# The first tile's row lookup, transposition and mean in a gathered expert FFN: two other orders of the same work

## The chip, the cores and the metric

The kernel runs on one core of a Trainium2 chip. The metric is the device time of one execution in microseconds (us). The core has five engines that each work through an instruction list of their own in order: TensorE (PE in the profile; its weight loads are listed apart as PEld), VectorE (DVE), ScalarE (ACT), GpSimd (POOL) and SyncE (SP). Transfers are issued by an engine's queue (here SP for the matrices, POOL for gathers and scatters by row number) and carried by 16 shared DMA engines. An engine waits for another, or for a transfer's landing, by semaphores.

## The reference

`x` is 4 x 512 tokens of 512 numbers, so 2048 rows. There are two stages.

```python
x = x + tanh(g_xattn) * moe(layernorm(x), ids, ctx)     # ctx[e]: the 512x512 matrix of expert e, used as Wg, Wu and Wd
x = x + tanh(g_ffn)   * ffn(layernorm(x), w1, w3, w2, wr)
```

In the first stage a token's expert (0 to 3) follows from its id alone, by the bounds 6250, 12500 and 18750. With its matrix M a normed row h gives `z = h M^T`, then `g = silu(z) * z`, then `y = g M^T`; all three weights are the same matrix. The second stage has three dense layers and adds gated rows of all tokens into 8 rows, one per route.

## The kernel before, in words

**Tiling.** Rows are sorted by expert into passes of 128 rows, 17 passes in all: 13 whole ones, each of one expert, and 4 mixed ones of four strips of 32 rows. `order` lists them; it begins 0, 1, 2, 3, 4. In this text x_p, m_p, h_p, z_p, g_p and y_p are the tiles of pass p: gathered rows, expert's matrix (1 MB), centred rows, and the products. The kernel is written with a manual schedule: each engine issues in the order of the program text, and a tile is waited for where it is first used.

**Sorting, L120 to L300.** DVE works out, for every token, its place among the sorted rows (`place`, L246; `padded`, L249), and splits it in a lane 0..127 (`lanes`, L251) and the pass's first place (`inpass`, L253). `which0` (L245) is the matrix of pass 0 alone, ready before the rest. The token number of every lane and pass is then found with matmuls: `atlane` (L258; columns 0..11 by `at_lane(0)`, columns 12..15 by `at_lane(1)`) has a one where a token sits in a lane, `what` (L267, L270; 128 x 17 x 16) has the token's number + 1 where it sits in a pass, and 16 matmuls (L276) add their products into `tok`, 128 lanes x 17 passes, in PSUM. `from_row` (L286) is `tok` as row numbers to gather. `later`, `stepped` and `which` (L287 to L300) give the matrix number of every pass, and `row_tables()` (L308 to L323, called at L836, behind them) gives `to_row` and `first`, seven short DVE instructions. PE meanwhile runs matmuls of ones whose results nobody reads, `busy(10)` before the lookup and `busy(21)` behind it (L200).

**Start of the passes, L846 on.** `load(p)` (L430) has SP read the pass's matrix number from SBUF and start the 1 MB transfer of m_p (L443). `gather(p)` (L387, DMA at L389) has POOL start the gather of x_p by `from_row`. Pass 0's matrix number is read from `which0`; the others are read from `held`, a copy of `which` that POOL makes (L849 for pass 1 alone, L854 for the rest). POOL's list at this place is: gather 0, copy for pass 1, gathers 1, 2, 3 and 4, copy for the rest. SP's list is: m_0, m_1 (which waits for the first copy), m_2 (which waits for the second copy), two loads of gates, m_3.

**First pass, `first_in` (L412).** DVE takes mean and variance of x_0 (L415, L417), subtracts the mean from each half of the columns (L422), PE transposes each half (L427), ACT copies it out of PSUM to hT (L428). `up` (L461) then multiplies: z_0 in four k steps of two matmuls each (L453), and between the third and the fourth k step PE transposes the next pass's centred rows (`turn_in`, L407, by L380 and L410). Behind z, ACT takes silu (L466) and DVE multiplies (L467), both with the row's inverse root `rs`, which `scale` makes in nine dependent DVE instructions on 128 x 1 numbers (L355 to L373). `centre(p)` (L397) is the mean and variance of a pass (L340, L342) and the subtraction (L401).

**Behind that** PE alternates the up and down products of the passes (L453) with transpositions (L380), fed by the same loads and gathers, and then the second stage's layers (L622, L730).

Of the kernel before, what the change touches and what calls it, by code (L numbers as in the profile page):

```python
# [19 lines left out]
P = 128  # L20
# [5 lines left out]
def tile_gated_moe_ffn(  # L26
# [40 lines left out]
    nc = tc.nc  # L67
    NT, D = x.shape
# [3 lines left out]
    KC = D // P  # L72
    NJ = NT // P
# [13 lines left out]
    work = ctx.enter_context(tc.tile_pool(name="work", bufs=3))  # L87
    small = ctx.enter_context(tc.tile_pool(name="small", bufs=4))
    ps_mm = ctx.enter_context(tc.tile_pool(name="ps_mm", bufs=2, space=bass.MemoryType.PSUM))
    ps_x = ctx.enter_context(tc.tile_pool(name="ps_x", bufs=2, space=bass.MemoryType.PSUM))  # L90
    ps_y = ctx.enter_context(tc.tile_pool(name="ps_y", bufs=1, space=bass.MemoryType.PSUM))
# [5 lines left out]
    on_the_way = {  # L97
        "lane", "atlane12", "atlane4", "passes", "what", "place", "over", "rank_in", "incl",
        "keep", "cum", "hot", "before", "later", "stepped", "behind", "ones", "place0", "number",
        "idt", "pad", "psum", "padded", "lanes", "inpass",  # L100
    }

    def ct_(shape, dtype, name):
        if name in on_the_way:
            return pos.tile(list(shape), dtype, tag=name, name=name)
        return const.tile(list(shape), dtype, tag=name, name=name)


    idt = ct_([P, NJ], I32, "idt")
# [28 lines left out]
    for e in range(1, E):  # L138
# [12 lines left out]
    H = 12  # L151
# [5 lines left out]
    number = ct_([P, NJ], F16, "number")  # L157
    nc.gpsimd.iota(
        number, pattern=[[1, NJ]], base=1, channel_multiplier=NJ,
# [13 lines left out]
    ident = ct_([P, P], F32, "ident")  # L173
# [66 lines left out]
    start = ct_([P, 2 * E - 1], F32, "start")  # L240
# [6 lines left out]
    padded = ct_([P, NJ], I16, "padded")  # L247
# [8 lines left out]
    def at_lane(h):  # L256
        j, n = (0, H) if h == 0 else (H, NJ - H)
        return nc.vector.tensor_tensor(  # L258
            atlane[h],
            lane[:, :, 0:n],  # L260
            lanes[:, j : j + n].unsqueeze(1).to_broadcast([P, P, n]),
            ALU.is_equal,
        )

    at_lane(0)
    what = ct_([P, NP, NJ], F16, "what")
    nc.vector.tensor_tensor(  # L267
        what, passes, inpass.unsqueeze(1).to_broadcast([P, NP, NJ]), ALU.is_equal
# [1 line left out]
    nc.vector.tensor_tensor(  # L270
        what, what, number.unsqueeze(1).to_broadcast([P, NP, NJ]), ALU.mult
    )
    at_lane(1)
    tok = ps_x.tile([P, NP], F32, tag="x", name="tok")
    for j in range(NJ):
        nc.tensor.matmul(  # L276
# [4 lines left out]
    later = ct_([P, 2 * E, NU], F32, "later")  # L281
    stepped = ct_([P, 2 * E - 1, NU], F32, "stepped")

    busy(21)
    from_row = ct_([P, NP], I32, "from_row")
    nc.vector.tensor_scalar(from_row, tok, -1.0, 0.0, ALU.add, ALU.max)  # L286
    nc.vector.tensor_tensor(  # L287
# [50 lines left out]
    def moments(xt, name):  # L338
        st = small.tile([P, 6], F32, tag="st", name=f"st_{name}")
        nc.vector.bn_stats(st, xt)  # L340
        mv = small.tile([P, 2], F32, tag="mv", name=f"mv_{name}")
        nc.vector.bn_aggr(mv, st)  # L342
        return mv
# [43 lines left out]
    def gather(p):  # L387
        xt = xp.tile([P, D], F32, tag="x", name=f"x_{p}")
        nc.gpsimd.indirect_dma_start(  # L389
            out=xt,  # L390
            out_offset=None,
            in_=x,
            in_offset=bass.IndirectOffsetOnAxis(ap=from_row[:, p : p + 1], axis=0),
        )
        xs[p] = xt

    def centre(p):  # L397

        mvs[p] = moments(xs[p], f"a{p}")
        hs[p] = work.tile([P, D], F32, tag="h", bufs=4, name=f"h_a{p}")  # L400
        nc.vector.tensor_scalar(hs[p], xs[p], mvs[p][:, 0:1], None, ALU.subtract)  # L401

    def scale(*ps):
        for p, rs in zip(ps, inverse_roots([mvs.pop(p) for p in ps], [f"a{p}" for p in ps])):
            rss[p] = rs
# [5 lines left out]

    def first_in(p):  # L412

        st = small.tile([P, 6], F32, tag="st", name=f"st_a{p}")
        nc.vector.bn_stats(st, xs[p])  # L415
        mvs[p] = small.tile([P, 2], F32, tag="mv", name=f"mv_a{p}")
        nc.vector.bn_aggr(mvs[p], st)  # L417
        hTs[p] = work.tile([P, KC * P], F32, tag="hT", bufs=2, name=f"hT_{p}")
        n = D // 2
        for i in range(2):  # L420
            h = work.tile([P, n], F32, tag="h", bufs=4, name=f"h_a{p}_{i}")
            nc.vector.tensor_scalar(  # L422
                h, xs[p][:, i * n : (i + 1) * n], mvs[p][:, 0:1], None, ALU.subtract
            )
            tp = ps_tp.tile([P, n], F32, tag="tp", name=f"tp_a{p}_{i}")
            for k in range(n // P):
                nc.tensor.transpose(tp[:, k * P : (k + 1) * P], h[:, k * P : (k + 1) * P], ident)  # L427
            nc.scalar.copy(hTs[p][:, i * n : (i + 1) * n], tp)  # L428

    def load(p):  # L430

# [413 lines left out]

    load(order[0])  # L846
    gather(order[0])
    one = slice(order[1], order[1] + 1)
    nc.gpsimd.tensor_copy(held[0:1, one], which[0:1, one])  # L849
    load(order[1])  # L850
    for i in range(1, 5):
        gather(order[i])
    rest = slice(order[1] + 1, NU)
    nc.gpsimd.tensor_copy(held[0:1, rest], which[0:1, rest])  # L854
    first_in(order[0])
    scale(order[0])
    centre(order[1])
    scale(order[1])
    load(order[2])
    nc.sync.dma_start(gates[:, 0:1], g_xattn.to_broadcast([P, 1]))  # L860
    nc.sync.dma_start(gates[:, 1:2], g_ffn.to_broadcast([P, 1]))
    load(order[3])
    up(order[0], inside=lambda: turn_in(order[1]))
    centre(order[2])
    scale(order[2])
    up(order[1], inside=lambda: turn_mid(order[0]))
    turn_in(order[2])
# [95 lines left out]
```

## Time and profile before

| what | value |
|---|---|
| median of 8 runs | 277.31 us (277.15 to 278.14) |
| the profiled execution: its own time | 277.26 us |
| its span, first to last instruction | 275.6 us |
| PE busy | 267.0 us, 97% of the span |
| DVE / ACT / POOL busy | 148.5 / 69.3 / 39.2 us |
| share of PE in the chain that ended last | 94% |
| mean granted TensorE clock | 0.996 |
| first matmul of z_0 | 15.13 us |

The profiled execution lies 0.05 us under the median, and 1.66 us of its time lie around its span. The timeline's columns are: start in us, duration in us, engine, line, operation, result<-operands, shapes, count, and in brackets the idle time of the engine just before and what ended it. Of a transfer started by a queue, the trace also has the landing: one record from each of the 16 DMA engines; a tile is usable when the last of them is in. In this trace the last records come, for m_0, at 11.47 us; for x_0 at 12.79, x_1 at 15.90, m_1 at 19.07, x_2 at 19.39, x_3 at 20.03, x_4 at 20.66 and m_2 at 24.32.

### The profile page before, as it was taken

How to read it: one execution, taken by the hardware profiler on the slowest of the kernel's cores; microseconds unless marked ns; L12 is line 12 of the kernel's file. 1: busy time of each engine (PE TensorE's matmuls, PEld its weight loads, DVE VectorE, ACT ScalarE, POOL GpSimd, SP SyncE). 2: the span in 40 equal slices, each digit the busy share in tenths (PEclk: the TensorE clock that was granted, in tenths of full speed). 3: DMA queues.
4: the chain of work that ended last, by engine and by line, in shares of the span. 5: the costliest groups of instructions: out<-in, count | busy, mean ns of one | idle time of the engine just before them, and what ended most of it. 6: DMA issues, size and time to landing. Idle time of an engine off the chain costs nothing.

```text
span 275.6 us, 3562 instructions
## 1 busy us (share of the span) xinstructions
PE 267.0 (97%) x1173; PEld 125.4 (46%) x1173; DVE 148.5 (54%) x593; ACT 69.3 (25%) x134; POOL 39.2 (14%) x63
## 2 busy tenths in 40 slices
PE   5889999999999999999999999999999999999994
PEld 2445455544355454444344444534345444344362
DVE  6687877877888779918263481516253620711000
ACT  2022232232233231233142232312113233301120
POOL 5520122221122211211110010101010000000000
PEclk9999999999999999999999999999999999999998
DMA  0797999545679996696213093001000000000000
GB/s 1 218 337 270 408 399 366 173 172 186 228 224 402 406 408 244 204 406 237 101 39 152 4 339 152 38 0 40 0 12 2 0 0 1 0 0 2 0 0 2
DMA packets 20722, 42.54 MB, mean 154 GB/s; under 512 B 2143, under 2 KB 2207, under 8 KB 20704
## 3 DMA queue, kind: packets, MB, share of 16 engines
q1 hardware_dynamic: 17952, 33.66, 34.3%
q0 software_dynamic: 2720, 8.65, 8.4%
q8 instruction: 9, 0.15, 0.2%
q14 instruction: 9, 0.07, 0.1%
q10 hardware_dynamic: 32, 0.01, 0.0%
HBM read 38.10 MB, written 4.47 MB: 154 GB/s over the span
## 4 chain that ended last, share of the span: by engine, by line
PE 94%; DVE 2%; DMA 2%; issue 1%; ACT 0%; DVEq 0%
PE z L453 22%; PE y L453 21%; PE v L730 20%; PE X L622 10%; PE Y L622 5%; PE tp_f L380 3%; PE tp_a L380 3%; PE tp_g L380 3%; PE Z L622 2%; PE acc L742 1%; PE lg L699 1%; DMA x<-in_x_dram,from_row 1%; DMA idt<-in_ids_dram 1%; PE accT L758 1%; PE o L814 0%
## 5 line engine op out<-in xcount | busy, mean ns | idle before, releaser
L453 PE MATMUL z<-m,hT 128*32 128x512 f32 (+1 forms) x232 | 61.9, 595 | 0.2 <-ACT hT L428 0.2
L453 PE MATMUL y<-m,gT 128*32 128x512 f32 (+1 forms) x232 | 61.4, 594 | 0.0
L730 PE MATMUL v<-w,s 128*128 128x512 f32 (+1 forms) x136 | 57.3, 570 | 0.0
L730 PEld LDWEIGHTS v<-w,s 128*128 128x128 f32 x136 | 25.0, 190 | 27.2 <-issue 26.7
L453 PEld LDWEIGHTS z<-m,hT 128*32 128x32 f32 (+1 forms) x232 | 22.6, 146 | 29.6 <-issue 28.1
L453 PEld LDWEIGHTS y<-m,gT 128*32 128x32 f32 (+1 forms) x232 | 22.6, 146 | 27.8 <-issue 27.8
L482 POOL DMA_INDIRECT out_dram<-x,to_row x17 | 17.2, 1010 | 86.2 <-DVE x L481 84.4
L389 POOL DMA_INDIRECT x<-in_x_dram,from_row x17 | 16.7, 980 | 76.0 <-DVE h_a L401 34.9
L467 DVE SCALAR_TENSOR_TENSOR g<-z,rs_a,g 128x512 f32<-128x512 f32 x17 | 12.8, 751 | 27.3 <-ACT g L466 27.3
L466 ACT ACTIVATE g<-z,rs_a 128x512 f32<-128x512 f32 x17 | 11.7, 687 | 51.3 <-PE z L453 51.0
L481 DVE SCALAR_TENSOR_TENSOR x<-y,tg,x 128x512 f32<-128x512 f32 x17 | 12.8, 750 | 18.9 <-PE y L453 18.9
L738 ACT ACTIVATE s<-v 128x512 f32<-128x512 f32 (+1 forms) x17 | 9.7, 572 | 41.9 <-PE v L730 41.9
L515 ACT COPY hT<-tp_f 128x512 f32<-128x512 f32 x13 | 7.6, 586 | 43.6 <-PE tp_f L380 43.6
L622 PE MATMUL X<-T,S 128*128 128x512 f32 x32 | 15.0, 592 | 0.0
L340 DVE BATCH_NORM_STATS2 st_a<-x 128x6 f32<-128x512 f32 x16 | 11.0, 687 | 5.0 <-DMA x<-in_x_dram,from_row 5.0
L380 PEld LDWEIGHTS tp_f<-ident,h_f 128*128 128x128 f32 x68 | 8.2, 141 | 10.2 <-issue 10.2
L340 DVE BATCH_NORM_STATS2 st_f<-x 128x6 f32<-128x512 f32 x17 | 11.8, 695 | 0.6
L380 PEld LDWEIGHTS tp_a<-ident,h_a 128*128 128x128 f32 x64 | 7.7, 141 | 9.4 <-issue 9.1
L640 DVE TENSOR_TENSOR s<-X,c 128x512 f32<-128x512 f32 x4 | 2.8, 692 | 16.2 <-PE X L622 16.2
L473 ACT COPY gT<-tp_g 128x512 f32<-128x512 f32 x17 | 10.0, 586 | 5.0 <-PE tp_g L380 5.0
L380 PE MATMUL tp_f<-ident,h_f 128*128 128x128 f32 x68 | 10.4, 276 | 0.0
L380 PE MATMUL tp_g<-ident,g 128*128 128x128 f32 x68 | 10.2, 273 | 0.0
(165 smaller groups left out, 271.8 us busy)
## 6 DMA issues: line engine op xcount, KB each, us to landing
m<-in_ctxT_dram SPq DMA_DIRECT2D x29, 1024.0 KB
w<-in_w1T_dram SPq DMA_DIRECT2D x1, 1024.0 KB
w<-in_w3T_dram SPq DMA_DIRECT2D x1, 1024.0 KB
w<-in_w2T_dram SPq DMA_DIRECT2D x1, 1024.0 KB
x<-in_x_dram,from_row POOLq DMA_INDIRECT x17, 6.0
out_dram<-x,to_row POOLq DMA_INDIRECT x17, 6.0
wr<-in_wrT_dram SPq DMA_DIRECT2D x1, 64.0 KB
x_first<-out_dram SPq DMA_DIRECT2D x4, 4.0 KB
```

Source lines behind the costliest of these rows:

```text
L340: nc.vector.bn_stats(st, xt)
L380: nc.tensor.transpose(tp[:, k * P : (k + 1) * P], h[:, k * P : (k + 1) * P], ident)
L389: nc.gpsimd.indirect_dma_start(out=xt, out_offset=None, in_=x, in_offset=bass.IndirectOffsetOnAxis(ap=from_row[:, p : p + 1], axis=0),)
L453: nc.tensor.matmul(out_ps[i * n : (i + 1) * n, :], lhs[:, k * P + i * n : k * P + (i + 1) * n], m[:, k, :], start=(k == 0), stop=(k == KC ...
L466: nc.scalar.activation(g, z, AF.Silu, scale=rs)
L467: nc.vector.scalar_tensor_tensor(g, z, rs, g, ALU.mult, ALU.mult)
L473: nc.scalar.copy(gT, tp)
L481: nc.vector.scalar_tensor_tensor(xt, y, tg[:, 0:1], xt, ALU.mult, ALU.add)
L482: nc.gpsimd.indirect_dma_start(out=out, out_offset=bass.IndirectOffsetOnAxis(ap=to_row[:, p : p + 1], axis=0), in_=xt, in_offset=None, bou ...
L622: nc.tensor.matmul(out_ps, a[:, k, c * P : (c + 1) * P], bb[:, k, :], start=start and k == 0, stop=k == 1, skip_group_check=True,)
L730: nc.tensor.matmul(v, s1[:, k, c_b + t * P : c_b + (t + 1) * P], w3[:, k, c0 : c0 + n], start=(k == 0), stop=(k == KC - 1),)
L738: nc.scalar.activation(s2, v, AF.Silu)
```

## The change

Two things are done in another way, and some of the work around them is put in another order.

1. The row numbers of pass 0 get a lookup of their own, ahead of the one for all passes. A 128 x 16 instruction makes `what0`, sixteen matmuls of one column make `tok0`, and a 128 x 1 instruction makes `from_row0`, by which gather 0 goes. The lookup for all 17 passes stays whole and comes behind it: its two instructions `what` now stand behind `from_row0` on DVE, its sixteen matmuls behind those of `tok0` on PE. The matmuls of ones behind it go from 21 to 11.
2. `first_in` transposes x_0 as it was gathered, and ACT copies the result to `raw`. DVE sums each row of x_0 (`total`), one matmul against the identity brings the sums, one per token, to all partitions of PSUM (`spread`), and two DVE instructions add `raw` and `spread` times -1/512 into hT, one for each half. Mean and variance of x_0, still needed for the inverse root, are taken behind that.
3. POOL's list becomes: gather 0, gather 1, copy for pass 1, gathers 2, 3, 4, copy for the rest. On DVE the order becomes: centre 1, inverse root of 0, centre 2, [g_0], inverse roots of 1 and of 2, [g_1]; before it was: root of 0, centre 1, root of 1, [g_0], centre 2, root of 2, [g_1]. SP's list, PE's order of products and ACT's list stay as they are.

```diff
+    what0 = ct_([P, NJ], F16, "what0")
+    nc.vector.scalar_tensor_tensor(what0, inpass, 0.0, number, ALU.is_equal, ALU.mult)
+    at_lane(1)
+    tok0 = ps_x.tile([P, 1], F32, tag="x", name="tok0")
+    for j in range(NJ):
+        nc.tensor.matmul(
+            tok0, atlane[j // H][:, :, j % H], what0[:, j : j + 1], start=(j == 0), stop=(j == NJ - 1)
+        )
+    from_row0 = ct_([P, 1], I32, "from_row0")
+    nc.vector.tensor_scalar(from_row0, tok0, -1.0, 0.0, ALU.add, ALU.max)
     what = ct_([P, NP, NJ], F16, "what")
...
-    at_lane(1)
     tok = ps_x.tile([P, NP], F32, tag="x", name="tok")
...
-    busy(21)
+    busy(11)
...
-            in_offset=bass.IndirectOffsetOnAxis(ap=from_row[:, p : p + 1], axis=0),
+            in_offset=bass.IndirectOffsetOnAxis(
+                ap=from_row0 if p == order[0] else from_row[:, p : p + 1], axis=0
+            ),
...
     def first_in(p):
-        st = small.tile([P, 6], F32, tag="st", name=f"st_a{p}")
-        nc.vector.bn_stats(st, xs[p])
-        mvs[p] = small.tile([P, 2], F32, tag="mv", name=f"mv_a{p}")
-        nc.vector.bn_aggr(mvs[p], st)
-        hTs[p] = work.tile([P, KC * P], F32, tag="hT", bufs=2, name=f"hT_{p}")
         n = D // 2
+        raw = work.tile([P, KC * P], F32, tag="h", bufs=4, name=f"raw_{p}")
         for i in range(2):
-            h = work.tile([P, n], F32, tag="h", bufs=4, name=f"h_a{p}_{i}")
-            nc.vector.tensor_scalar(
-                h, xs[p][:, i * n : (i + 1) * n], mvs[p][:, 0:1], None, ALU.subtract
-            )
             tp = ps_tp.tile([P, n], F32, tag="tp", name=f"tp_a{p}_{i}")
             for k in range(n // P):
-                nc.tensor.transpose(tp[:, k * P : (k + 1) * P], h[:, k * P : (k + 1) * P], ident)
-            nc.scalar.copy(hTs[p][:, i * n : (i + 1) * n], tp)
+                c = i * n + k * P
+                nc.tensor.transpose(tp[:, k * P : (k + 1) * P], xs[p][:, c : c + P], ident)
+            nc.scalar.copy(raw[:, i * n : (i + 1) * n], tp)
+        total = small.tile([P, 1], F32, tag="total", name="total")
+        nc.vector.tensor_reduce(total, xs[p], AX.X, ALU.add)
+        spread = ps_y.tile([P, P], F32, tag="y", name="spread")
+        nc.tensor.matmul(spread, total.to_broadcast([P, P]), ident, start=True, stop=True)
+        hTs[p] = work.tile([P, KC * P], F32, tag="hT", bufs=2, name=f"hT_{p}")
+        for i in range(2):
+            half = slice(i * n, (i + 1) * n)
+            nc.vector.scalar_tensor_tensor(
+                hTs[p][:, half].rearrange("p (k t) -> p k t", t=P),
+                spread.unsqueeze(1).to_broadcast([P, n // P, P]),
+                -1.0 / D,
+                raw[:, half].rearrange("p (k t) -> p k t", t=P),
+                ALU.mult,
+                ALU.add,
+            )
+        mvs[p] = moments(xs[p], f"a{p}")
...
     load(order[0])
     gather(order[0])
     one = slice(order[1], order[1] + 1)
+    gather(order[1])
     nc.gpsimd.tensor_copy(held[0:1, one], which[0:1, one])
     load(order[1])
-    for i in range(1, 5):
+    for i in range(2, 5):
         gather(order[i])
...
     first_in(order[0])
+    centre(order[1])
     scale(order[0])
-    centre(order[1])
-    scale(order[1])
+    centre(order[2])
     load(order[2])
...
     up(order[0], inside=lambda: turn_in(order[1]))
-    centre(order[2])
+    scale(order[1])
     scale(order[2])
     up(order[1], inside=lambda: turn_mid(order[0]))
```

More of the change, by code (lines that the diff above doesn't have):

```diff
@@ L99, in tile_gated_moe_ffn @@
         "keep", "cum", "hot", "before", "later", "stepped", "behind", "ones", "place0", "number",
-        "idt", "pad", "psum", "padded", "lanes", "inpass",
+        "idt", "pad", "what0", "psum", "padded", "lanes", "inpass",
     }
```

## Prediction

> **What bounds the kernel now.** The first view is the chain that ended last: PE holds 94% of it. The second is that chain in order of time over the first 30 us, for where it isn't PE:
>
> ```profile
> 7.86 1.00 PE tok L276 x16
> 9.35 3.44 DMA x<-in_x_dram,from_row
> 12.81 0.70 DVE st_a L415
> 13.76 0.36 DVE h_a L422
> 14.26 0.42 PE tp_a L427 x2
> 14.71 0.38 ACT hT L428
> 15.13 2.84 PE z L453 x6
> 17.97 0.44 PE tp_a L380 x4
> 18.41 3.61 PE z L453 x8
> 22.02 0.44 PE tp_g L380 x4
> ```
>
> Up to 15.13 us a chain of short steps decides. From there PE runs on; behind 20 us I find no distance between matmul starts that tells of a wait until the last microseconds. So whatever moves the start of z_1 moves the end by as much, and what is won before that can still be lost at z_1. Eight matmuls at 0.43 us make 3.44, and the row at 18.41 shows 3.61: z_1 already waited there. The third view, the timeline around it, shows for whom:
>
> ```profile
> 11.16 0.39 SPq L443 DMA_DIRECT2D m<-in_ctxT_dram  x1
> ...
> 18.45 0.58 ACT L410 COPY hT<-tp_a 128x512 f32<-128x512 f32 x1 [3.10 <-PE tp_a L380]
> ...
> 19.18 0.30 PEld L453 LDWEIGHTS z<-m,hT 128*128 128x128 f32 x2 [0.74 <-ACT hT L410]
> ```
>
> hT of pass 1 is there at 19.03, m_1's last landing record is 19.07, and z_1's first matmul starts at 19.21, 0.14 behind it. z_0's last matmul starts at 18.68 and holds PE until 19.11. The trace names ACT, but **m_1 lands as late as z_1 can bear**. The windows of 1 us say why a late issue can't be made up: from 14 us on the DMA engines are full (the last two columns are their busy share and GB/s).
>
> ```profile
> 12.00:13.00 1.00, 1.00 (x7) 0.41 (x5) 0.19 (x1) 0.00 (x0) 0.90 (x1) 1.00 0.83 129
> 13.00:14.00 1.00, 0.38 (x2) 0.00 (x0) 0.93 (x3) 0.00 (x0) 0.69 (x2) 1.00 0.68 213
> 14.00:15.00 1.00, 0.65 (x4) 0.40 (x4) 0.90 (x6) 0.29 (x2) 0.69 (x2) 1.00 0.97 330
> 15.00:16.00 1.00, 0.87 (x2) 0.49 (x3) 0.85 (x5) 0.35 (x2) 0.74 (x2) 1.00 1.00 338
> 16.00:17.00 1.00, 1.00 (x4) 0.43 (x3) 0.94 (x3) 0.00 (x0) 0.00 (x0) 1.00 0.99 328
> 17.00:18.00 1.00, 1.00 (x5) 0.47 (x4) 0.90 (x4) 0.00 (x0) 0.00 (x0) 1.00 1.04 414
> ```
>
> **Part 1, the lookup of pass 0.** `what0` takes the place of `what` at 7.11. It has 16 numbers, like `inpass` (0.16 us), and the matmuls follow at about 7.33, where `busy(10)` ends (3.18 + 4.13 = 7.31); before they began at 7.86. The sixteen take 0.99 in the trace (7.86 to 8.85), paced by their weight loads, so one column costs about as much as 17. `tok0` is there at 8.30, `from_row0` runs 8.34 to 8.49, and with the 0.29 between `from_row`'s end (9.06) and the gather (9.35), gather 0 starts at 8.78, **0.57 earlier**. With its 3.44 us x_0 lands at 12.22, not 12.79; m_0's transfer, in until 11.47, may take back a part.
>
> What this pushes back is everything else on DVE. `what` and its product now start behind `from_row0`: 8.41 to 8.70, and 8.80 to 9.10 (0.29, 0.30, and the step of 0.39 between them at 7.11 and 7.50). The matmuls of `tok` follow at 9.16, end at 10.14, and `from_row` starts at 10.17, where it was 8.88: **1.29 later**. DVE works in order, so `later`, `stepped`, `which` and the seven instructions of `row_tables()` move along: `which` ends at 10.33 + 1.29 = 11.62 and `first` begins at 12.78, so that the next instruction can start at about 12.98.
>
> **Part 2, first_in.** The ones end at about 12.4 (from 10.0, 11 x 0.2155 = 2.37), the four transposes take 0.65, the two copies end 0.65 behind their start, at about 13.5: hidden, because DVE comes later. `total` reads 512 numbers. A reduction of 203 takes 0.53, and the line through the reductions of 7 (0.153) and 203 reaches 1.12; I take 0.69, the BATCH_NORM_STATS2 of the same tile. It ends at 13.67. PE follows 0.14 later (as 14.12 to 14.26), the `spread` matmul costs 0.28 like a transpose or 0.39 with a second pass, as z has two to a k step; with 0.39 it ends at 14.20. The first half of hT is 256 numbers with one operand in PSUM: L422 took 0.37 for 256 without PSUM, L401 0.49 for 512, and half of L467's 0.75 with PSUM is 0.38; I take 0.41. Then z_0 starts at 14.24 + 0.41 + 0.04 = 14.69, **0.44 earlier** (0.0 with the slow reduction, 0.6 with the quick one). Mean and variance of x_0, 0.69 + 0.18, go behind hT, off the path. z_0 took 3.98 from first matmul to PE free (15.13 to 19.11), so z_1 could start at 18.67.
>
> Is the rest ready by then? x_1 is gathered at 10.35 + 0.29 = 10.64 (before 10.82). DVE then has hT to 15.0, moments of x_0 to 15.8, centre 1 to about 17.2, and the transposes in z_0 come at 14.69 + 2.68 = 17.4: just in time. rs_0, nine instructions or 1.85 us (14.33 to 16.18), is ready at about 19.0, ACT takes silu to 19.7, centre 2 to 20.3, g_0 to 21.0; it is needed 2.65 behind z_1's start, 21.3 at the earliest. All hidden.
>
> **Part 3, the order on POOL, and who waits behind it.** Gather 1 needs `from_row`, now at 10.35, and holds POOL from 10.64 to 11.62. The copy for pass 1 needs `which`, also 11.62, where it was 10.33. It starts at about 11.7 and ends at 11.9 (0.18); SP waits for it and issues 0.49 later, as 10.67 to 11.16 before. **m_1 is issued at about 12.35, 1.2 us later.** Behind the copy stand gathers 2 to 4, some 0.2 us later than before; behind m_1 on SP m_2, the gates and m_3, as late as the gathers, with slack (m_2 landed at 24.32, z_2 begins at 27.46).
>
> When does m_1 land? From issue to last landing m_0, alone, took 5.34 us (6.13 to 11.47), m_1 7.91 (11.16 to 19.07), m_2 8.09 (16.23 to 24.32). A gather in front of it costs 0.64 (x_2, x_3 and x_4 land at 19.39, 20.03, 20.66). In the changed kernel x_1 should be over when m_1 begins, but x_2 now stands to m_1 as x_1 did, issued just before it, and x_3 as x_2 did. So the nearest row is m_1 itself, 7.91. It is 2.57 above m_0's, four gathers' worth, and x_1 to x_4 were about; now three are left, which would be 5.34 + 1.93 = 7.27. I take 7.6, between the two: 12.35 + 7.6 = 19.95. The ends are 17.7 (m_0's time) and 20.4 (m_2's).
>
> [...]
>
> **The sum.** z_1 starts at 19.95 + 0.14 = 20.09 instead of 19.21: +0.88. The 0.44 won before it becomes idle PE time. The profiled execution's 277.26 becomes 278.14; the median of the runs stood 0.05 higher. I say **278.1 us**. About 0.2%, 0.55 us, is what a measurement of this kernel can tell from no change.
>
> **Rivals.**
> - *m_1 late, but by less* (lands at 18.7 to 19.6). For it: the DMA engines were only 0.68 to 0.83 busy from 12 to 14, and x_0 and x_1 go out sooner. Against it: m_1 and m_2 both took about 8 us. z_1 starts at 18.85 to 19.75: -0.35 to +0.55, 276.9 to 277.8.
> - *The start is won, the kernel is faster.* The mechanism is at z_1: m_1 is issued late but has the engines nearly to itself, and decides nothing from a landing at 18.55 or earlier, that is 6.2 us behind its issue; m_0 took 5.34. Then z_0's gain passes whole: 277.3 less 0.4 to 0.65, 276.65 to 276.9. g_0 is next late: with x_2 landing at 19.4 as before, centre 2 holds g_0 until 21.5 and 0.2 goes.
> - *PE's clock falls.* PE is now nearly empty from 7.3 to 9.95, from 12.4 to 14.7 and while z_1 waits. Before, the clock stayed at 1.00 with gaps of 0.54 and 0.88. [...] If it falls, it may stay down as at the start, where the ones took 0.43 and not 0.2155 from 3.18 to 7.31: half of these 4.1 us lost, +2, about 279.3.
> - *No earlier start at all*: `total` at 1.12 puts z_0 at 15.1. Behind a late m_1 that changes nothing, so it is part of the forecast.
>
> **How the numbers follow.** Forecast (m_1 lands behind 19.6) 0.53, m_1 less late 0.22, won 0.20, clock 0.05. The won case is split at 276.76: 0.12 faster, 0.08 within 0.2%. Faster 0.12, within 0.30, slower 0.58. The range, 276.7 to 278.7, takes in the ends of m_1's landing and leaves out the clock and the best of the won case.
>
> **What would show it.** Right: gather 0 near 8.8, z_0's first matmul near 14.7, m_1's issue near 12.3, an idle gap of PE over 1 us ahead of z_1, z_1 near 20.1, and the same PE order at the same pace from there. Wrong: m_1 in by 18.6, or m_1's issue hardly moved (then POOL's copy doesn't wait for `which` as I say), or any row of z_0 at twice 0.43.

## The result, and the profile after

The changed kernel takes 278.99 us (median of 21 runs, 278.06 to 281.75). The kernel before took 277.67 us beside it (60 runs, 277.01 to 278.5). The ratio is 1.006, with a 95% interval of 1.0048 to 1.0072: **slower by 0.6%**, 1.3 to 2.0 us. The profiled execution took 279.68 us, of which 278.0 are its span; before, the span was 275.6. Here and below a ratio goes by the executions within 1.5% of the fastest of their kernel, which leaves out two of twelve in late_copy and four of twelve in two_ahead.

The first view is again the chain that ended last, in order of time (start in us, duration, what). Its piece at 12.06 is new:

```profile
9.88 0.19 DVE from_row L296
10.06 0.26 issue
10.32 0.95 POOL x L399
...
11.40 0.18 POOL held L872
...
12.06 8.94 DMA m<-in_ctxT_dram
20.99 0.14 issue
21.13 2.81 PE z L475 x6
```

Before, no transfer of a matrix was on this chain. Now the path runs from `from_row` over gather 1 on POOL, the copy behind it and SP to m_1, issued at 12.06 (before 11.16), and z_1 starts 0.14 behind m_1's last landing. The timeline of PE shows what was waited for:

```profile
9.68 4.22 PE L200 MATMUL idle<-ones 128*128 128x512 bf16 x11
13.73 0.60 PE L433 MATMUL tp_a<-ident,x 128*128 128x128 f32 x4
14.17 0.39 PE L438 MATMUL spread<-ident,total 128*128 128x128 f32 x2
15.14 2.84 PE L475 MATMUL z<-m,hT 128*128 128x512 f32 x6 [0.59 <-DVE hT L442]
...
21.13 2.81 PE L475 MATMUL z<-m,hT 128*128 128x512 f32 x6 [1.84 <-DMA m<-in_ctxT_dram]
```

z_0 starts at 15.14, where it started at 15.13: nothing of the earlier gather (8.54 us instead of 9.35) is left. z_1 starts at 21.13 instead of 19.21, 1.92 late. The first row says where z_0's gain went. Eleven matmuls of ones take 4.22 us, 0.43 each for most of them where before they took 0.22, so PE is not through with them before 13.73. In the windows below (busy us of PE, PEld, DVE, ACT, POOL, then the granted clock, the DMA share and GB/s) the clock is down for 3.4 us, just there:

```profile
7.00:10.28 3.28, 2.49 (x37) 2.12 (x36) 1.46 (x7) 0.00 (x0) 1.26 (x1) 1.00 1.00 292
10.28:13.70 3.42, 3.42 (x9) 1.29 (x8) 2.76 (x11) 0.00 (x0) 2.80 (x4) 0.50 0.80 191
13.70:15.14 1.44, 0.86 (x7) 0.63 (x5) 0.47 (x2) 0.65 (x2) 1.14 (x2) 1.00 0.66 189
```

Matmul for matmul, after lags before by 1.92 us from z_1 to 93 us and by 2.41 from 98 us to the end. The second step, 0.49, lies at the first z of the pass of strips near 95 us, which waits for the last of its four matrices.

### The profile page after: what moved, and what is told of

Same layout as the page of the kernel before. It is cut to its first block, busy times and chain, and to the rows that moved or that the text cites. A ratio compares the mean times of both kernels' runs of the same rounds, so it can differ in the third digit from the quotient of the medians.

```text
span 278.0 us, 3578 instructions
## 1 busy us (share of the span) xinstructions
PE 267.9 (96%) x1181; PEld 126.5 (46%) x1181; DVE 149.1 (54%) x596; ACT 69.3 (25%) x134; POOL 39.6 (14%) x63
## 4 chain that ended last, share of the span: by engine, by line
PE 93%; DMA 4%; DVE 1%; POOL 0%; issue 0%; SPq 0%; POOLq 0%
PE y L475 21%; PE z L475 20%; PE v L752 20%; PE X L644 10%; PE Y L644 5%; DMA m<-in_ctxT_dram 3%; PE tp_f L390 3%; PE tp_g L390 3%; PE tp_a L390 3%; PE Z L644 2%; PE idle L200 1%; PE acc L764 1%; PE lg L721 1%; PE accT L780 1%; DMA idt<-in_ids_dram 1%; PE o L836 0%
## 5 line engine op out<-in xcount | busy, mean ns | idle before, releaser
L350 DVE BATCH_NORM_STATS2 st_a<-x 128x6 f32<-128x512 f32 x17 | 11.7, 687 | 8.5 <-DMA x<-in_x_dram,from_row 8.5
```

## The experiments

**The theories.** *1:* m_1 is issued late, lands late, and z_1 moves the end. *2:* PE's clock falls behind the early lookup, and PE is late by that. *3:* the new `first_in` and DVE's new order cost. *4:* waits far behind, near 95 and 104 us, cost. *5*, formed later: the new tile `from_row0` moves the tiles behind it in SBUF, and transfers get slower by their address.

Each ratio below is to the kernel before on the same chip, and the kernels of a group ran on one chip, after on the first. "Late" is how much later than in the profile of before z_1 starts, and how much more is added at the pass of strips. "Clock" counts, among the executions compared, those whose mean granted clock is 0.994 or lower, a lower bound for the falls (fourth group); in the 147 executions of the kernel before beside these it never was under 0.995.

| kernel | ratio, 95% interval | m_1 issued, landed | z_0 | z_1 late | strips | clock |
|---|---|---|---|---|---|---|
| after | 1.0060 (1.0048 to 1.0072) | 12.06, 20.99 | 15.14 | 1.92 | 0.49 | 15 of 21 |
| late_copy | 1.0011 (0.9985 to 1.0037) | 12.43, 19.80 | 15.09 | 0.73 | 0 | 0 of 10 |
| which_early | 1.0019 (0.9996 to 1.0043) | 11.04, 19.28 | 15.01 | 0.52 | 0.25 | 8 of 12 |
| hold_clock | 1.0007 (0.9979 to 1.0035) | 12.08, 19.40 | 14.43 | 0.32 | 0.70 | 0 of 12 |
| both | 1.0035 (1.0015 to 1.0055) | 10.84, 16.95 | 13.95 | 0.20 | 0 | 0 of 12 |
| change_again | 1.0039 (1.0014 to 1.0064) | 12.31, 19.62 | 16.39 | 1.16 | 0.76 | 7 of 12 |
| lookup_alone | 1.0063 (1.0039 to 1.0088) | 12.31, 19.80 | 15.34 | 0.72 | 0.69 | 6 of 6 |
| first_in_alone | 0.9999 (0.9975 to 1.0024) | 11.17, 19.27 | 14.69 | 0.20 | 0 | 0 of 12 |
| gathers_held | 1.0035 (1.0006 to 1.0064) | 12.27, 19.14 | 15.35 | 0.11 | 0 | 7 of 12 |
| later_copy | 1.0144 (1.0113 to 1.0175) | 15.03, 22.23 | 15.15 | 3.16 | 0 | 3 of 6 |
| two_ahead | 1.0011 (0.9984 to 1.0037) | 11.88, 19.89 | 15.32 | 0.82 | 0.67 | 2 of 8 |
| more_matmuls | 1.0005 (0.9982 to 1.0027) | 11.18, 18.39 | 15.46 | 0.23 | 0 | 0 of 12 |
| change_third | 1.0050 (1.0025 to 1.0075) | 12.33, 19.79 | 14.68 | 0.72 | 1.07 | 5 of 12 |
| hold_clock_again | 1.0059 (1.0034 to 1.0084) | 12.29, 19.92 | 14.63 | 0.84 | 0.87 | 0 of 9 |
| clock_and_gathers | 1.0032 (1.0007 to 1.0057) | 12.39, 20.00 | 14.74 | 0.93 | 0.57 | 0 of 12 |
| no_ones | 1.0052 (1.0032 to 1.0072) | 11.20, 20.00 | 15.72 | 1.81 | 0 | 9 of 11 |
| shifted | 1.0015 (0.9991 to 1.0039) | 11.01, 18.27 | 15.29 | 0.93 | 0.49 | 0 of 12 |
| change_aligned | 1.0048 (1.0021 to 1.0075) | 12.30, 20.80 | 15.20 | 1.72 | 0.18 | 11 of 12 |
| both_aligned | 1.0003 (0.9984 to 1.0023) | 11.07, 17.36 | 14.13 | 0.21 | 0.11 | 0 of 12 |

Not every late z_1 waited for m_1. In which_early, both, both_aligned and shifted PE waited inside z_0 (0.56, 1.29, 1.12 and 0.69 us) to transpose h_1, because x_1 came late. In change_again, gathers_held, no_ones and more_matmuls z_1 follows a z_0 that itself started late. Behind z_1, PE's lag to the kernel before changes in these profiles at two places only: at the strips and, in 15 of them, near 104 us, where PE stops for 1.1 to 2.0 us (third group). The table has no column for that stop, which is as large as what is looked for; the profiles of before, after, both, first_in_alone and two_ahead don't have it.

### First group: m_1's issue or the clock

**late_copy**: the kernel before, with the change's order on POOL and nothing else of it.

```diff
     load(order[0])
     gather(order[0])
     one = slice(order[1], order[1] + 1)
+    gather(order[1])
     nc.gpsimd.tensor_copy(held[0:1, one], which[0:1, one])
     load(order[1])
-    for i in range(1, 5):
+    for i in range(2, 5):
```

> The kernel before, with one thing of the change: POOL's copy of pass 1's matrix number stands behind gather 1, so m_1 is issued later, at about 12.2 us instead of 11.16. Lookup, first_in and the matmuls of ones are untouched. Theory 1 (m_1's late landing is the loss): the landing moves with the issue or more, z_1 starts at 20.1 to 21.1 instead of 19.2, and the time is 0.9 to 1.9 us above before, 278.6 to 279.6. Theory 2 (the fall of TensorE's clock, seen in the profile of the changed kernel from 10.3 to 13.7, is the loss): the clock stays at 1.00, time as before, 277.7. Theory 3 (the new order on DVE and first_in are the loss): as before, 277.7.

**which_early**: the change, with `from_row` made behind `later`, `stepped` and `which` on DVE, and the copy for pass 1 ahead of gather 1 on POOL again.

```diff
-    from_row = ct_([P, NP], I32, "from_row")
-    nc.vector.tensor_scalar(from_row, tok, -1.0, 0.0, ALU.add, ALU.max)
...
+    from_row = ct_([P, NP], I32, "from_row")
+    nc.vector.tensor_scalar(from_row, tok, -1.0, 0.0, ALU.add, ALU.max)
...
-    gather(order[1])
     nc.gpsimd.tensor_copy(held[0:1, one], which[0:1, one])
+    gather(order[1])
```

> The changed kernel, with later, stepped and which moved ahead of from_row on DVE, into the time in which it waits for the lookup's matmuls, and POOL's copy for pass 1 ahead of gather 1 again. m_1 should be issued at about 10.7 us instead of 12.06. Theory 1 (m_1's late landing): m_1 lands at 18.6 to 19.6, z_1 starts at 19.1 to 19.7, time within 0.5 us of before, 277.6 to 278.2; the clock still falls and z_0 still starts at 15.1. Theory 2 (the clock): unchanged, 279.0. Theory 3 (order on DVE, first_in): unchanged, 279.0.

**hold_clock**: the change with `busy(3)`, three matmuls of ones, between the sixteen of `tok0` and the sixteen of `tok`.

> The changed kernel, with three more matmuls of ones between the 16 of tok0 and the 16 of tok, where PE sat idle for 0.8 us. The clock should then not fall at 10.3, the ones should end at 12.4 and z_0 start at 14.2 to 14.4 instead of 15.14. Theory 1 (m_1's late landing): z_1 still waits for m_1 until about 21, time as the changed kernel, 279.0. Theory 2 (the clock): 0.8 us or more faster than the changed kernel, 278.2 or less. If the clock falls all the same, it isn't the idle 0.8 us that lets it fall.

**both**: the edits of which_early and hold_clock together.

> The changed kernel with both edits: which ahead of from_row with the copy ahead of gather 1, and three more matmuls of ones. Theory 1: z_0 starts at 14.2 to 14.4 and could be through at 18.3; m_1, issued at 10.7, lands at 18.6 to 19.6 and decides, so z_1 starts at 18.8 to 19.7: 277.2 to 278.1, at best 0.4 us faster than before. Theory 2: z_1 follows z_0 at 18.3, 0.9 us faster than before, 276.8. Theory 3: 279.0.

*Measured, and what follows.* The profile of late_copy does what theory 1 says: m_1 is issued at 12.43, 1.27 later than before, and z_1 follows its landing. So does that of hold_clock. In which_early and both m_1 is early again, and z_1 waits for x_1 instead. The times tell little here. Three of the four intervals hold 1, and both, whose profile has the earliest z_0, has the highest ratio. On this chip the runs of before spread from 276.9 to 279.9 us, where they spread by 1.5 us on the first. The profile of both, 277.51 us, has no stop near 104 us, and ten of its other eleven executions lie 1.8 to 2.6 us above it, about what such a stop and a wait at the strips come to; so its ratio and its profile tell of different executions.

### Second group: which part of the change carries it

**change_again**: the changed kernel once more.

> The changed kernel itself, for the same chip as the runs beside it. Theory 1 (m_1's late landing): m_1 issued at 12.1 lands at 19.4 to 21.0, z_1 starts at 19.5 to 21.1, 0.3 to 1.9 us above before. In the profiles so far m_1 took 6.1 to 8.9 us from issue to landing, so one profile alone does not settle the size. Theory 4 (a later wait of PE, at the first pass of strips near 94 us or at the router's matmuls near 104 us, where the profiles of four kernels show 0 to 1.8 us): PE is late by more at the end than at z_1.

**lookup_alone**: the kernel before with the lookup of pass 0, POOL's order and `busy(11)`; `first_in` and DVE's order behind it stay as before.

```diff
+    what0 = ct_([P, NJ], F16, "what0")
...
+    from_row0 = ct_([P, 1], I32, "from_row0")
+    nc.vector.tensor_scalar(from_row0, tok0, -1.0, 0.0, ALU.add, ALU.max)
...
-    busy(21)
+    busy(11)
...
+    gather(order[1])
...
-    for i in range(1, 5):
+    for i in range(2, 5):
```

> The kernel before with the lookup of pass 0 ahead, POOL's new list and 11 matmuls of ones, but with the old first_in and the old order on DVE. DVE reaches first_in at about 12.6, x_0 lands at 12.2, so z_0 starts at about 15.0, as before, if the matmuls of ones end in time; if the clock falls they end at 13.7, still ahead of the transposes at 14.0. Theory 1: m_1 is issued at 12.1 and z_1 starts at 19.5 to 21.1: 0.3 to 1.9 us slower than before, like the whole change. Theory 3 (first_in and the order on DVE): as before.

**first_in_alone**: the kernel before with the change's `first_in` and its order on DVE, with the old lookup and POOL's old order.

```diff
     first_in(order[0])
-    scale(order[0])
     centre(order[1])
-    scale(order[1])
+    scale(order[0])
+    centre(order[2])
...
-    centre(order[2])
+    scale(order[1])
     scale(order[2])
```

> The kernel before with the new first_in and the new order on DVE, but the old lookup, POOL's old list and 21 matmuls of ones. m_1 is issued at 11.16 as before. The ones end at 13.4 and hold the transposes of x_0 until then; spread follows at 14.0 and z_0 starts at about 14.8. Theory 1: m_1 lands at about 19.1, z_1 at 19.2, time within 0.3 us of before; the 0.3 won at z_0 is idle time ahead of z_1. Theory 3: as slow as the whole change, 1.3 us or more above before.

**gathers_held**: the change, with gathers 3 and 4 held back until DVE is through with centre 1 (it copies their row numbers to a tile of their own).

```diff
-    for i in range(2, 5):
-        gather(order[i])
+    gather(order[2])
...
     centre(order[1])
...
+    nc.vector.tensor_copy(later_row, from_row[:, 3:5])
+    gather(order[3])
+    gather(order[4])
```

> The changed kernel with gathers 3 and 4 held back behind centre 1 (their row numbers are copied by DVE there), so that only x_2 goes out near m_1. If the gathers behind it are what makes m_1 take 7.3 to 8.9 us, it should land 6.0 to 6.7 us behind its issue at 12.1, at 18.1 to 18.8, and z_1 should follow z_0 at about 19.1: within 0.3 us of before (277.7 where the whole change has 279.0). If m_1's own transfer is slow, z_1 stays at 19.5 to 21.1 and the time as that of the whole change.

*Measured, and what follows.* first_in_alone is at 0.9999, lookup_alone at 1.0063: the lookup with its order carries the loss, and theory 3 falls. The timeline of first_in_alone shows the new `first_in` doing what it should, with a win that stops at the same door:

```profile
14.69 2.84 PE L463 MATMUL z<-m,hT 128*128 128x512 f32 x6 [0.59 <-issue]
...
19.41 1.96 PE L463 MATMUL z<-m,hT 128*128 128x512 f32 x4 [0.26 <-DMA m<-in_ctxT_dram]
```

z_0 is 0.44 earlier, by `first_in` alone; z_1 waits for m_1, which lands at 19.27. In gathers_held m_1 took 6.87 us and z_1 was 0.11 late, and yet the ratio is 1.0035: something behind z_1 counts as well. In its profile that is the stop near 104 us, 1.95 us.

### Third group: the dose, and a lookup for two passes

**later_copy**: the kernel before, with the copy for pass 1 behind gathers 1, 2 and 3.

```diff
+    for i in range(1, 4):
+        gather(order[i])
     nc.gpsimd.tensor_copy(held[0:1, one], which[0:1, one])
     load(order[1])
-    for i in range(1, 5):
-        gather(order[i])
+    gather(order[4])
```

> The kernel before, with the copy for pass 1 behind gathers 1, 2 and 3 on POOL: m_1 is issued at about 14.9 us instead of 11.16, 3.7 later, three times the delay of the changed kernel. Theory 1 (z_1 waits for m_1 and the rest follows z_1): m_1 lands at 22 to 23, z_1 starts 2.9 to 3.9 later than before, and the time is about as much above before, 281.7 to 282.7 where before has 278.8. Theory 4 (the time is set by later waits at 94 and 104 us, which absorb or add by themselves): the difference at the end is not that at z_1; if those waits absorb, it is under 2 us.

Its timeline:

```profile
15.15 2.84 PE L453 MATMUL z<-m,hT 128*128 128x512 f32 x6 [0.24 <-ACT hT L428]
...
22.37 1.96 PE L453 MATMUL z<-m,hT 128*128 128x512 f32 x4 [3.07 <-DMA m<-in_ctxT_dram]
```

No lookup, no new `first_in`, the same clock until z_1: m_1 is issued 3.87 later, z_1 starts 3.16 later and the kernel is slower by 1.44%, 4.0 us (1.13% to 1.75%). An issue of m_1 that comes late reaches the end, and the mechanism of theory 1 is shown by that. The three executions that kept the clock have a mean of 282.37, 3.0 us above the median of before, about z_1's 3.16; the three others have 283.82, and no profile shows where these lose 1.4 more.

**two_ahead**: which_early and hold_clock, and a lookup that gives the row numbers of passes 0 and 1 together, so that gather 1 too goes ahead.

```diff
-    what0 = ct_([P, NJ], F16, "what0")
-    nc.vector.scalar_tensor_tensor(what0, inpass, 0.0, number, ALU.is_equal, ALU.mult)
+    what0 = ct_([P, 2, NJ], F16, "what0")
+    for i in range(2):
+        nc.vector.scalar_tensor_tensor(
+            what0[:, i, :], inpass, float(i * P), number, ALU.is_equal, ALU.mult
+        )
```

> The changed kernel with the clock held (three matmuls of ones between the lookups), which ahead of from_row, and the early lookup made for passes 0 and 1, so that gather 1 follows gather 0 at once and the copy for pass 1 comes behind it, without a wait. Gather 1 at about 9.8, x_1 landing at 13.0, m_1 issued at about 11.4, and z_0 from 14.0. Theory 1: m_1 lands 6.1 to 7.4 behind its issue, at 17.5 to 18.8; z_0 is through at 18.0; z_1 starts at 18.1 to 18.9 and the time is 0.3 to 1.1 us below before. Theory 4: the wait at 104 us adds 1.5 to 2 us in most runs, as in the runs of the kernel with both edits, and the median is above before all the same.

The median of all twelve is 280.45 us in a wide spread (277.79 to 283.38); the ratio is that of eight and can't be told from 1. Its profile wins nothing: z_1 is 0.82 late, since m_1 took 8.01 us.

**more_matmuls**: the kernel before with eight more small matmuls of ones, for the number of PE's instructions alone.

```diff
     busy(21)
+    for _ in range(8):
+        nc.tensor.matmul(idle[:, 0:64], ones, ones[:, 0:64], start=True, stop=True)
```

> The kernel before with eight more small matmuls of ones behind the 21, in PE's idle time ahead of x_0's transposes: PE's instruction count is that of the changed kernel (1181 against 1173), nothing else is. Theory 1: as before, within 0.2 us; z_1 at 19.2. Theory 4 in the form that the wait at the router's matmuls depends on where they fall in PE's instruction stream: the median goes up by 0.5 to 1.5 us, and the profile, if it falls on such a run, shows pauses at 103 to 106 us that wait for nothing shown.

It is about theory 4. In 15 of the 20 profiles of this study the router's matmuls (`lg`) stop twice between 103 and 107 us, and the shift to before grows there by 1.1 to 2.0 us. The rows of more_matmuls name no cause:

```profile
102.28 1.85 PE L701 MATMUL lg<-hT,wr 128*32 128x128 f32 x48
104.48 0.40 PE L701 MATMUL lg<-hT,wr 128*32 128x128 f32 x2 [0.35 <-issue]
105.22 0.69 PE L701 MATMUL lg<-hT,wr 128*32 128x128 f32 x14 [0.34 <-issue]
```

"issue" is a wait for nothing that the profile shows. The stop is there in kernels that hardly differ from before (this one, late_copy, shifted) and isn't in the profile of after, so it is no part of the 2.41 us between the two profiles. The number of PE's instructions isn't its cause, since late_copy and shifted have as many as before. What causes it stays open, and that it comes and goes may be what spreads the medians of the later groups.

### Fourth group: the clock by itself

**change_third**: the changed kernel, beside the next three.

> The changed kernel again, beside the next three. Theory 1 (m_1's late landing): m_1 is issued near 12.2 us and lands between 19.1 and 21.0; z_1 starts 0.14 behind it; the ratio to the kernel before is 1.003 to 1.006. Theory 2 (clock): the clock falls to 0.5 for one stretch of 3.41 us between 10 and 15, and z_0 starts at 15.1 or later. Both may hold. Theory 4 (later waits): PE waits again near 95 or 104 us, and less than half of the loss is there at z_1.

**hold_clock_again**: hold_clock, on this chip.

> The change with three matmuls of ones between the two lookups, so that PE isn't thin there. Theory 2: the clock stays at 1.00, z_0 starts near 14.4, and the ratio is lower than that of the change by 0.002 or more. Theory 1: z_0 starts near 14.4 too, but z_1 still follows m_1's landing at 19.4 or later, and the ratio stays within 0.002 of the change's.

**clock_and_gathers**: the edits of hold_clock and gathers_held together.

> The change with the three matmuls of ones, and with gathers 3 and 4 held back until DVE is through with centre 1. If theories 1 and 2 are both needed: the clock stays, z_0 starts near 14.4, m_1 takes 6.9 us or less and lands by 19.1, z_1 starts at 18.5 to 19.2, and the time is within 0.3 us of the kernel before's or up to 0.5 under it (ratio 0.998 to 1.001). Theory 4: z_1 is as early as before or earlier, and the time is still 0.6 us or more above (ratio 1.002 or more), by waits near 95 or 104 us.

**no_ones**: the kernel before without its 21 matmuls of ones behind the lookup.

```diff
-    busy(21)
+    busy(0)
```

> The kernel before without the 21 matmuls of ones behind the lookup; nothing else is changed. Theory 2: PE is empty from 8.9 to 14.3, the clock falls to 0.5 and is still there when z_0 begins; z_0's matmuls take 0.85 instead of 0.43 for part of the pass, z_1 starts 0.9 to 3.4 us later than 19.2, and the end follows by as much (ratio 1.003 to 1.012), though m_1 lands where it did. If the clock's price is hidden behind m_1's landing: z_1 starts within 0.3 of 19.2 and the ratio is below 1.002.

*Measured, and what follows.* The clock's price can be seen where it falls late enough. In no_ones PE has nothing to do from 8.89 to 14.60, the clock is at 0.5 from 11.58 to 18.41, and z_0's first six matmuls take 4.16 us instead of 2.84:

```profile
15.72 4.16 PE L453 MATMUL z<-m,hT 128*128 128x512 f32 x6
20.15 2.82 PE L453 MATMUL z<-m,hT 128*128 128x512 f32 x6
```

Behind it z_1 starts 1.81 us late, and the ratio is 1.0052. Not all of that is the clock: m_1 landed at 20.00 here and would have held z_1 until 20.14, so 0.88 of the 1.81 comes on top of m_1. In the profile of the changed kernel the clock falls earlier, and only the ones are slow (eleven in 4.22 us; the four transpositions behind them take 0.60). With `busy(3)` the mean clock shows a fall in none of 57 executions of four kernels (hold_clock, both, clock_and_gathers, both_aligned), though two_ahead, which has it too, shows one in 2 of the 8 compared and in 6 of all 12. The loss was not smaller with the clock held: 1.0059 beside change_third's 1.0050. The timeline of hold_clock_again is the forecast almost to the row:

```profile
14.63 2.84 PE L476 MATMUL z<-m,hT 128*128 128x512 f32 x6 [0.59 <-DVE hT L443]
17.75 1.02 PE L476 MATMUL z<-m,hT 128*128 128x512 f32 x2
20.05 2.81 PE L476 MATMUL z<-m,hT 128*128 128x512 f32 x6 [1.28 <-DMA m<-in_ctxT_dram]
```

The executions, parted by their mean clock, show next to no price either. Of the changed kernel's 21 on the first chip, 6 kept the clock by this measure (0.995 or more): their median is 278.96 us, 1.29 above the median of before; the 15 others' is 279.19. Within change_again the 7 with a fallen clock have a mean of 279.67 and the 5 others 279.91; within change_third it is 280.32 (5) and 280.60 (7).

That parting is weaker than it looks. The profiled execution of change_again, with a mean clock of 0.998, counts among the 5 others, and its timeline is that of a slow clock:

```profile
9.93 4.85 PE L200 MATMUL idle<-ones 128*128 128x512 bf16 x11
...
16.39 2.84 PE L475 MATMUL z<-m,hT 128*128 128x512 f32 x6 [0.59 <-DVE hT L442]
...
19.51 3.68 PE L475 MATMUL z<-m,hT 128*128 128x512 f32 x8
```

All its matmuls of ones take some 0.43 us, the ten ahead of the lookup and these eleven, and the trace's first record of the clock is a full one at 15.41. The mean, 0.998, does not show a clock that has not risen yet. So the counts of fallen clocks are lower bounds, and "kept" is sure only where a profile shows it. Here z_1 followed z_0 at 20.37 without a wait, where m_1, in at 19.62, would have let it start at 19.76: the clock cost 0.6 us at z_1.

So theory 2 is true as a mechanism (0.88 us on top of m_1 in no_ones, 0.6 at z_1 in change_again), and on the chip where hold_clock_again and change_third stood side by side it is not the cause of most of the loss: behind a late m_1 most of its price is hidden.

clock_and_gathers held the clock and moved two gathers away, and m_1 still took 7.61 us. SP's next load had moved up into the gap: m_2 was issued at 13.71 instead of 16.16. Two gathers went from beside m_1 and a load came; whether that is why m_1 was no faster was not tried.

### Fifth group: the address

The pass of strips was late, by 0.25 to 1.07 us, in 9 of the 11 profiles with the new lookup so far, and in none of the 6 with the old one. The lookup adds one lasting tile, `from_row0`, and by the programs' own allocation the matrices start 32 bytes later in every partition (64 in the two kernels that hold gathers; before, at byte 93952). The view of the DMA queues between 93 and 100 us, where the DMA engines are full (a busy share of 1.04 in before from 92 to 96 us and 1.06 from 96 to 100), had the 2 KB packets of SP's queue slower wherever that was so. Three kernels try it.

**shifted**: the kernel before with `from_row` 32 bytes longer.

```diff
-    from_row = ct_([P, NP], I32, "from_row")
+    from_row = ct_([P, NP + 8], I32, "from_row")[:, 0:NP]
```

> The kernel before, with from_row made 32 bytes longer, so that all tiles behind it, the matrices and gathered rows among them, start 32 bytes later in SBUF, as in the change; nothing else differs. Theory 5 (the address): between 93 and 100 us a 2 KB packet takes 87.4 to 88.4 ns on average, where it took 84.4 to 84.9; the strip pass near 94 us waits 0 to 1 us for its last matrix, since z_1 is not late; ratio 1.001 to 1.004. If the address is nothing: 84.4 to 84.9 ns, no wait, ratio within 0.0015 of 1.

**change_aligned**: the change with `from_row0` among the sorting's tiles, which leaves all addresses behind it as before.

```diff
-        "idt", "pad", "what0", "psum", "padded", "lanes", "inpass",
+        "idt", "pad", "what0", "from_row0", "psum", "padded", "lanes", "inpass",
```

> The change, with from_row0 kept among the sorting's tiles, so that matrices and gathered rows lie at the same addresses as in the kernel before. Theory 5: packets at 84.4 to 84.9 ns, no wait of the strip pass, ratio 0.0015 to 0.003 below the change's 1.004 to 1.006. Theory 1 (m_1's late landing): z_1 still starts 0.5 to 1.2 us late, at 19.7 to 20.4, and what is left of the ratio is 1.0015 to 1.004. If the address is nothing: 87.4 to 88.4 ns, and the ratio stays at 1.004 to 1.006.

**both_aligned**: the same edit in both.

> The variant with three matmuls of ones between the lookups and the matrix numbers made ahead of from_row, with from_row0 again among the sorting's tiles. If m_1's issue, the clock and the address are the whole loss: m_1 is issued near 10.9, z_1 starts at 18.5 to 19.5, packets at 84.4 to 84.9 ns, ratio 0.997 to 1.0005. If something else is left: z_1 no later than 19.5 and a ratio of 1.002 or more.

*Measured.* The queue that carries the matrices, 93 to 100 us, in before, shifted, change_third and change_aligned (packets, MB, and the time of its packets as a share of 16 engines):

```profile
q1 hardware_dynamic: 1187, 2.37, 87.8%
```
```profile
q1 hardware_dynamic: 1306, 2.60, 99.8%
```
```profile
q1 hardware_dynamic: 1220, 2.42, 93.3%
```
```profile
q1 hardware_dynamic: 1288, 2.56, 94.5%
```

A share of 16 engines' 7 us over the MB: 0.878 x 112 / 2.37 = 41.5 us of an engine's time for a MB in before, 43.0 in shifted, 43.2 in change_third, 41.3 in change_aligned. All 20 profiles fall in these two groups: 41.3 to 41.6 in the eight with the addresses of before, 42.8 to 43.3 in the twelve with 32 or 64 bytes more. **That the address makes these packets 4% slower is shown.** The same figure between 30 and 40 us parts the profiles in the same way, 42.3 to 43.4 and 44.3 to 46.6. Between 14 and 22 us, where gathers run between the matrices, it doesn't (43.8 to 50.0 and 43.9 to 49.0), so nothing here says that the address delayed m_1. Why 32 or 64 bytes cost this much is not shown, and no other step was tried.

The wait of the strips goes with it: it averages 0.55 us over the twelve and 0.04 over the eight. That it is worth as much in the whole time is not shown. shifted is at 1.0015 with an interval that holds 1, and change_aligned at 1.0048, no lower than the change.

*What follows from the pair.* On one chip, change_aligned is at 1.0048 (1.0021 to 1.0075) and both_aligned at 1.0003 (0.9984 to 1.0023); both profiles have the stop near 104 us, and their spans, 278.8 and 277.4, differ by z_1's 1.5 us less 0.1 behind it. They differ by `busy(3)` and by `which` and its copy going ahead again, so the two edits together take the loss away. Since `busy(3)` alone took nothing away on the chip where change_third stood beside it, what is left of the pair is m_1's issue, 11.07 instead of 12.30. That step is argued and not shown: no kernel on this chip changes m_1's issue alone, late_copy, which does, stayed at 1.0011 (0.9985 to 1.0037), and the same two edits without the alignment were at 1.0035. Theory 1 stands as the mechanism, by later_copy and by the chain of the changed kernel; how much of the median's loss it makes is not settled. No kernel here beats the one before, though, and both_aligned's profile shows why a start of 14.13 brings nothing:

```profile
18.10 0.63 PE L391 MATMUL tp_a<-ident,h_a 128*128 128x128 f32 x4 [1.12 <-DVE v_a L366]
18.56 2.82 PE L476 MATMUL z<-m,hT 128*128 128x512 f32 x6
```

m_1 goes out at 11.07, 0.34 behind gather 1 (10.73), and DVE waits 1.29 for x_1, until 16.52; in after, where m_1 goes out 1.74 behind gather 1, x_1 is in at 13.67. In these profiles an m_1 close behind gather 1 goes with a late x_1. h_1 is ready at 17.95 and transposed at 18.10 (the view names v_a, DVE's next instruction), where z_0 wanted it at 16.8. z_1 starts at 19.42 all the same.

## Why the prediction was wrong

The direction and the mechanism were right: m_1 is issued late because the copy waits behind gather 1 and `which`, z_1 waits for it, and the start's gain turns into idle PE. The time, 278.1, was too low, and 278.99 lies above the range. Two terms of the sum were too small. The delay of z_1, put at 0.88, was 1.92 in the profiled execution, because m_1 took 8.93 us from issue to landing and not 7.6. What comes behind z_1 was put at nothing ("the same pace from there"), and it was 0.49.

- **Part 1** held. Gather 0 went at 8.54 (forecast 8.78), x_0 landed at 12.16 (12.22), `which` ended at 11.32 (11.62), and m_1 was issued at 12.06 (12.35), at 12.31 and 12.33 in the next two profiles.
- **Part 2** held in its sizes: `total` took 0.68 (0.69), and z_0 started at 14.68 in change_third and 14.69 in first_in_alone (14.69). It failed in the profiled execution, where the ones ended not at 12.4 but at 13.73. What failed there is the clock: the rival that lets it fall had 0.05, the author's own estimate, which no run bears out: with the new lookup and no ones added it fell in at least 59 of 87 executions of five kernels. Nor does the rival's picture describe this fall: PE was not nearly empty but busy for 2.49 of the 3.28 us ahead, with no idle stretch above 0.79. The rival's price failed too: not +2 but nothing at z_1 in the profiled execution, where the clock fell ahead of z_0 and m_1 came later still, and 0.6 in that of change_again.
- **Part 3** is the term that was mis-sized in the profiled execution. Issue to landing was put at 7.6, with ends at 5.34 and 8.09; it was 8.93. Ten profiles have m_1 issued between 12.06 and 12.43; there it took 6.87 to 8.93, with a median of 7.5, and z_1 was a median of 0.78 late, where 0.88 was forecast. So the value was good and the end was not: it came from three transfers of one execution. What makes m_1 take 6.87 in one execution and 8.93 in another stays open.
- **"From there the same pace"** failed. The strips add 0.49, a wait that the trace of before didn't have: their last matrix landed 0.7 us ahead of its first use there (92.92, 93.6); in after it lands at 95.96, 0.46 behind the first z of that pass. No step of the prediction looked at what a new tile does to the addresses of the others.
- **The sum.** In the profiled execution 1.92 and 0.49 make the span's 2.41. For the medians, 0.8 from z_1 and half a microsecond from the strips make 1.3, the lower end of what was measured (1.3 to 2.0). That sum isn't settled term by term: the strips' share in the whole time was not resolved, and hold_clock gave 1.0007 on one chip and 1.0059 on another. A rival is open too: the stop near 104 us, absent from the profiles of before and after, is in both later profiles of the changed kernel (1.9 and 1.4 us), and how many executions without a profile have it is not known, so the 1.3 may hold some of it. The fastest executions of the two kernels, 277.01 and 278.06, still lie 1.05 apart. The base moved as well: 277.67 beside the changed kernel, not 277.31, and the forecast's 0.88 on that base would be 278.55.
- **Rivals.** "No earlier start" was true of the profiled execution, by the clock and not by a slow `total`. "The start is won" needed a landing 6.2 us behind the issue, which none of the ten had.

## What to carry to other kernels

A start that comes earlier is worth what the next late transfer leaves of it: before a copy that a load waits for is moved behind anything, read when that load's data are used, and put the load's spread over several executions in the range (6.87 to 8.93 us for m_1 in ten profiles here), not its duration in one. Matmuls of ones that seem to fill a gap may be holding the clock (without the 21 of them it was at 0.5 from 11.58 to 18.41 us in no_ones), and a mean clock near 1 doesn't prove that it was up from the start (0.998 in change_again). A small lasting tile moves all tiles behind it (by 32 bytes here, with packets 4% slower from 93 to 100 us), so compare addresses when a stretch with full DMA engines slows down and nothing in it was changed.

## What the runs showed of the hardware that was not expected

- The clock fell although PE was busy for 2.49 us of the 3.28 ahead, most of that with matmuls of 1 and 17 columns. In the profile of after it fell for one stretch of 3.41 us; by the mean clock it fell in some executions and not in others of the same kernel (15 of 21 of after), and with three matmuls of ones (0.65 us) between, the mean clock showed no fall in 57 executions of four kernels, though it did in 6 of 12 of a fifth, two_ahead.
- Packets into SBUF took 4% longer with the matrices 32 or 64 bytes further on, from 93 to 100 us, where the DMA engines were full (42.8 to 43.3 us of an engine for a MB, 41.3 to 41.6 before).
- The same 1 MB load, issued within 0.4 us of the same time (12.06 to 12.43) in ten profiles, took from 6.87 to 8.93 us.
- Dense small matmuls stopped twice near 104 us in 15 of 20 profiles, with no wait in the profile to name (PE idle for 0.35 and 0.34 us in more_matmuls); the lag to before grew there by 1.1 to 2.0 us.
- A clock that had not risen by 15.41 us in change_again (the eleven matmuls of ones took 4.85 us from 9.93, some 0.43 each) left a mean granted clock of 0.998.
